# Language ids packed in the opening, and read into registers in fours

## The chip, the cores and the metric

The kernel runs on one core of a Trainium2 chip. Its engines work side by side, each through its own instructions in a fixed order: TensorE (PE in the profile, with its weight loads apart as PEld), VectorE (DVE), ScalarE (ACT), GpSimd (POOL) and SyncE (SP), which here issues transfers. They wait for each other by semaphores. The metric is the device time of one execution in microseconds, as the median of several runs.

## The reference

128 batches of 128 rows by 512 columns, float32. Each batch b has a language id from 0 to 8, and the id picks that batch's weights out of ten sets: a down projection W1 (512 to 128) with bias and relu, an up projection W2 (128 to 512) with bias, then a layer norm with a gamma and a beta of that language. Two residuals are added.

```python
w1 = W1[language_ids]
w2 = W2[language_ids]
h = jnp.einsum('bsh,bha->bsa', hidden_states, w1) + b1[language_ids][:, None, :]
h = jax.nn.relu(h)
adapted = jnp.einsum('bsa,bah->bsh', h, w2) + b2[language_ids][:, None, :]
x = hidden_states + adapted
mean = jnp.mean(x, axis=-1, keepdims=True)
var = jnp.mean(jnp.square(x - mean), axis=-1, keepdims=True)
normed = (x - mean) * jax.lax.rsqrt(var + LN_EPS)
return normed * gamma[language_ids][:, None, :] + beta[language_ids][:, None, :]
```

The output is the input x plus that result. The ids are data of the run, not known when the program is built.

## The kernel before

One batch is one tile of 128 by 512, and a loop written out over 128 batches passes it from engine to engine. TensorE transposes x (`transpose_x`, L479), multiplies by the batch's W1 (`down`, L502) and, after ScalarE's bias and relu (L510), by W2 (`up`, L524). VectorE adds the residual and sums (`residual`, L542), scales by gamma (`scale`, L608), takes the root through three small Newton steps (L579, L581, L584) and ends the batch (`finish`, L617). ScalarE copies the transposed tile (L483), squares (L565) and takes the root (L575). GpSimd adds b2 and beta to x ahead of time (`add_b2`, L489; `add_beta`, L496). SP loads x by pairs of batches (L188) and stores pairs (L621). Five PSUM banks hold the products of `up`; a bank is free again when `finish` of its batch has run.

The tables of all languages lie in the core's memory, so an id becomes an address: the offset of a slice of w2, beta_b, gamma_b, b2_b or w1. For that the engine that uses it needs the id in a register of its own. An engine gets it by a read (`TENSOR_LOAD`, L271), which stands in its order like any other instruction; one read can fill several registers.

The first 20 ids (NEAR) are read from the tile `lang`, four at a time, shortly before they are used. The other 108 are packed first: four ids of five bits, times 512, into one of 27 integers of the tile `packed`. VectorE does that with four small operations (`pack_ids`, L265 to L268). Each of the five engines then reads all 27 integers in one go (`read_packed`, L278) and keeps them in registers for the rest of the run; `lid` and `lid_h` take an id out by a shift and a mask.

The opening, up to batch 4, is a list of calls. After it the order on all engines follows a plan: every step is entered with a due time counted in batches, and the steps are sorted by it. Packing is due at 4.5, the long reads at 5.8 (SP), 6.7 (GpSimd), 7.6 (ScalarE), 8.5 (TensorE) and 9.4 (VectorE). In the opening VectorE also spreads the rows of beta and part of b2 over all 128 partitions (`shuffle_rows`, L397, 17 shuffles), and GpSimd's first `add_beta` waits for these.

Of the kernel before, what the change touches and what calls it, by code (L numbers as in the profile page):

```python
# [13 lines left out]
ET = mybir.EngineType  # L14
# [3 lines left out]
G = 4  # L18
# [125 lines left out]
def cond_resid_kernel(ctx: ExitStack, tc: tile.TileContext, x, itok, W1, b1, W2, b2, gamma, beta, out):  # L144
# [9 lines left out]
    B, S, H = x.shape  # L154
# [8 lines left out]
    def keep(ins):  # L163

        engine = ins.ins.engine
        if engine in last:
            tc.add_manual_dep(ins.ins, last[engine], behind, reason="kept order")
        last[engine] = ins.ins.name
        return ins
# [21 lines left out]
    def xb(b):  # L191
        return xs[b // X][:, b % X, :]


    ids = const.tile([1, B], I32, name="ids")
# [50 lines left out]
    lids, w1s = {}, {}  # L246
# [8 lines left out]
    NEAR, BITS = 20, 5  # L255
    FAR = (B - NEAR) // 4
    assert L <= 1 << BITS and H == 1 << 9 and NEAR % G == 0 and NEAR + 4 * FAR == B
    packed = const.tile([1, FAR], I32, name="packed")

    def pack_ids():  # L260

        def part(k):
            return lang[:, NEAR + k * FAR : NEAR + (k + 1) * FAR]

        keep(nc.vector.scalar_tensor_tensor(packed, part(3), float(1 << BITS), part(2), ALU.mult, ALU.add))  # L265
        for k in (1, 0):
            keep(nc.vector.scalar_tensor_tensor(packed, packed, float(1 << BITS), part(k), ALU.mult, ALU.add))
        keep(nc.vector.tensor_scalar(packed, packed, float(H), 0.0, ALU.mult, ALU.add))  # L268

    def read_ids(tile, engine, most, why):  # L270
        loads, vals = nc.values_load_multi_w_load_instructions(  # L271
            tile, engines=[engine], min_val=0, max_val=most, skip_runtime_bounds_check_because=why
        )
        for ins in loads:
            keep(ins)
        return vals

    def read_packed(engine):  # L278
        lids["far", engine] = read_ids(
            packed, engine, ((1 << 4 * BITS) - 1) * H, "four ids of 0..L-1 at five bits each, times H"  # L280
        )

    def near(b, engine):
        g = b // G
        if (g, engine) not in lids:
            lids[g, engine] = read_ids(
                lang[0:1, g * G : (g + 1) * G], engine, L - 1, "clamped on the chip to 0..L-1 above"
            )
        return lids[g, engine][b % G]

    def lid(b, engine):
        if b < NEAR:
            return near(b, engine)
        k, i = divmod(b - NEAR, FAR)
        v = (lids["far", engine][i] >> (BITS * k + 9)) & ((1 << BITS) - 1)
        return v.with_bounds(min_val=0, max_val=L - 1)

    def lid_h(b, engine):

        if b < NEAR:  # L300
            return near(b, engine) * H
        k, i = divmod(b - NEAR, FAR)
        v = lids["far", engine][i]
        if k:
            v = v >> (BITS * k)
        v = v & (((1 << BITS) - 1) * H)
        return v.with_bounds(min_val=0, max_val=(L - 1) * H, guaranteed_mod_val=0, out_of_modulus=H)
# [4 lines left out]
    def load_first(b):  # L312
        w1s[b] = wp.tile([P, KC, A], FP, tag="w1s", name=f"w1s_{b}")
        src = W1[bass.ds(lid(b, ET.SP), 1)].rearrange("o (p k) a -> p (o k a)", k=KC)
        keep(nc.sync.dma_start(out=w1s[b].rearrange("p k a -> p (k a)"), in_=src))
# [49 lines left out]
    def transpose_b1():  # L365
        b1p = p_h.tile([P, P], FP, tag="h", name="b1p")
        keep(nc.tensor.transpose(b1p[:, :L], b1r, ident[:L, :L]))
        keep(nc.vector.tensor_copy(b1T, b1p[:, :L]))
# [6 lines left out]
    def spread(r, copier):  # L375
        t = (beta_b, gamma_b, b2_b)[r // L]
        row = p_y.tile([P, H], FP, tag="y", name=f"row_{r}")
        pick_r = pick[:, r : r + 1].to_broadcast([96, P])
        keep(nc.tensor.matmul(row, lhsT=pick_r, rhs=parts[:96, :], start=True, stop=True))
        dst = t[:, r % L * H : (r % L + 1) * H]  # L380
        if copier is nc.scalar:
            keep(nc.scalar.copy(dst, row))
        else:
            keep(nc.vector.tensor_copy(dst, row))
# [53 lines left out]
    def load_rows(b):  # L438
        w1s[b] = wp.tile([P, KC, A], FP, tag="w1s", name=f"w1s_{b}")
        rows = W1[bass.ds(lid(b, ET.SP), 1)].rearrange("o (i k r) a -> i (o r) k a", i=4, k=KC)  # L440
        for i in range(4):
            keep(nc.sync.dma_start(out=w1s[b][32 * i : 32 * (i + 1)], in_=rows[i]))
# [21 lines left out]
    def stage_w1(b):  # L464
        w1s[b] = wp.tile([P, KC, A], FP, tag="w1s", name=f"w1s_{b}")
        gpsimd = turn(b) == "c"
        v = lid_h(b, ET.Pool if gpsimd else ET.Activation)
        src = w1.rearrange("p l k a -> p (l k a)")[:, bass.ds(v, KC * A)]
        dst = w1s[b].rearrange("p k a -> p (k a)")
        keep(nc.gpsimd.tensor_copy(dst, src) if gpsimd else nc.scalar.copy(dst, src))  # L470

    def transpose_x(b):
        pxs[b] = p_x.tile([P, KC, P], FP, tag="xT", name=f"pxT_{b}")
        for k in range(KC):
            if b < EARLY:
                cols = xb(b).rearrange("s (p k) -> s k p", k=KC)[:, k, :]
            else:
                cols = xb(b)[:, k * P : (k + 1) * P]
            keep(nc.tensor.transpose(pxs[b][:, k, :], cols, ident))  # L479

    def copy_xT(b):
        xT[b] = tp.tile([P, KC, P], FP, tag="xT", name=f"xT_{b}")
        keep(nc.scalar.copy(xT[b], pxs.pop(b)))  # L483

    def add_b2(b):
        if b2_on_gpsimd(b):
            rs[b] = rp.tile([P, H], FP, tag="r", name=f"r_{b}")
            v = lid_h(b, ET.Pool)
            keep(nc.gpsimd.tensor_tensor(rs[b], xb(b), b2_b[:, bass.ds(v, H)], ALU.add))  # L489

    def add_beta(b):
        g, j = divmod(b, 2)
        if g not in os:
            os[g] = op.tile([P, 2, H], FP, tag="o", name=f"o_{g}")
        v = lid_h(b, ET.Pool)
        keep(nc.gpsimd.tensor_tensor(os[g][:, j, :], xb(b), beta_b[:, bass.ds(v, H)], ALU.add))  # L496
# [11 lines left out]
    def relu(b):  # L508
        hT[b] = tp.tile([P, P], FP, tag="hT", name=f"hT_{b}", bufs=5)
        keep(nc.scalar.activation(hT[b], phs.pop(b), AF.Relu, bias=b1T[:, bass.ds(lid(b, ET.Activation), 1)]))  # L510
# [228 lines left out]
    def spin(n, width):  # L739
        idle = p_s.tile([P, H], FP, tag="s", name="idle")  # L740
        for _ in range(n):
            keep(
                nc.tensor.matmul(
                    idle[:, :width], lhsT=ones, rhs=ones[:, 0:1].to_broadcast([P, width]), start=True, stop=True
                )
            )
# [3 lines left out]
    def x_turn(b):  # L750
        transpose_x(b)
        copy_xT(b)
# [3 lines left out]
    spread(10, nc.scalar)  # L756
    spin(1, H)
    x_turn(0)
    transpose_b1()
    spread(11, nc.scalar)  # L760
    for n in (0, G):
# [16 lines left out]
    relu(2)  # L778
    spread(18, nc.scalar)
    spread(19, nc.scalar)  # L780
    add_beta(0)
    add_beta(1)
    spread(20, nc.scalar)
# [13 lines left out]
    def at(when, step, *args):  # L797
        plan.append((when, len(plan), step, args))
# [39 lines left out]
    for g in range(E // 2 - 1):  # L838
        b = 2 * g
# [13 lines left out]
            at_pair(g, when("scale", b) + 0.001, lid, b + G, ET.DVE)  # L853
        at_pair(g, when("store", b), store, g)

    at(4.5, pack_ids)
    for n, engine in enumerate((ET.SP, ET.Pool, ET.Activation, ET.PE, ET.DVE)):
        at(4.5 + 1.3 + 0.9 * n, read_packed, engine)

    for _, _, step, args in sorted(plan, key=lambda step: step[:2]):  # L860
        step(*args)
# [185 lines left out]
```

## Time and profile before

| | us |
|---|---|
| median of 3 runs | 303.61 |
| lowest and highest | 302.27, 303.68 |
| profiled execution | 303.65 |
| its span, first to last instruction | 300.9 |

| engine | busy us | share of the span |
|---|---|---|
| TensorE | 290.9 | 97% |
| VectorE | 291.2 | 97% |
| ScalarE | 273.4 | 91% |
| GpSimd | 276.2 | 92% |

Times inside the profile count from the first instruction. Reads into registers, register arithmetic and the issue of transfers are not counted as busy, so an engine that stands still for a read shows as idle. What the profile names as the end of an idle time is the semaphore that came last, which need not be the cause. The profiled execution is 2.75 us longer than its span.

### The profile page before, as it was taken

The page shows a single profiled execution, that of the slowest core. Times are in us where ns is not written, and L with a number is a line of the kernel's source. Part 1 is how long each engine was busy: PE and PEld are TensorE (multiplying, and loading weights), DVE is VectorE, ACT ScalarE, POOL GpSimd, SP SyncE. Part 2 cuts the span into 40 slices and gives each one's busy share as a digit, 9 for nine tenths or more (in the row PEclk, how much of TensorE's full clock was granted, in tenths as well). Part 3 has the DMA queues.
Part 4 walks back from the last instruction along what each step waited for, and adds up shares of the span by engine and source line. Part 5 has one row for each costly group of instructions (what it writes and reads, how often), then busy time and mean ns, then how long its engine had stood idle before and what let it go on. Part 6 is the DMA issues. An engine that isn't in the chain of part 4 may idle for free. (4 is left out here: it accounts for less than half of the span.)

```text
span 300.9 us, 8471 instructions
## 1 busy us (share of the span) xinstructions
PE 290.9 (97%) x1779; PEld 216.2 (72%) x1779; DVE 291.2 (97%) x780; ACT 273.4 (91%) x760; POOL 276.2 (92%) x238
## 2 busy tenths in 40 slices
PE   7998899999999999999999999999999999999993
PEld 3866587777767787777777777777777777777760
DVE  5999999999999999999999999999999999999995
ACT  4975688999999999999999999999999999899992
POOL 1196998999999999999999999999999999999982
PEclk9999999999999999999999999999999999999999
DMA  6999999969779898859975997949976898993816
GB/s 230 390 387 365 323 337 360 376 200 261 259 235 304 253 405 262 319 177 319 370 249 220 257 394 263 342 140 321 392 236 243 260 343 286 290 367 117 278 42 238
DMA packets 62260, 85.80 MB, mean 285 GB/s; under 512 B 4186, under 2 KB 26213, under 8 KB 62211
## 3 DMA queue, kind: packets, MB, share of 16 engines
q1 hardware_dynamic: 62150, 85.23, 83.8%
q8 instruction: 15, 0.25, 0.3%
q14 instruction: 35, 0.28, 0.3%
q10 hardware_dynamic: 60, 0.05, 0.1%
HBM read 51.71 MB, written 33.55 MB: 283 GB/s over the span
## 5 line engine op out<-in xcount | busy, mean ns | idle before, releaser
L496 POOL TENSOR_TENSOR o<-x,beta_b 128x512 f32<-128x512 f32 x121 | 151.9, 1278 | 15.4 <-DVE beta_b L397 12.7
L502 PEld LDWEIGHTS ph<-xT,w1s 128*128 128x128 f32 x1024 | 126.9, 192 | 13.4 <-ACT hT L510 8.3
L502 PE MATMUL ph<-xT,w1s 128*128 128x128 f32 x1024 | 135.4, 275 | 0.1
L489 POOL TENSOR_TENSOR r<-x,b_b 128x512 f32<-128x512 f32 x83 | 105.0, 1278 | 2.2 <-DVE part L581 1.6
L524 PE MATMUL py<-w,hT 128*128 x196 | 100.6, 596 | 1.5 <-DVE o L617 1.4
L479 PEld LDWEIGHTS pxT<-ident,x 128*128 128x128 f32 x464 | 60.1, 151 | 54.3 <-issue 39.5
L608 DVE SCALAR_TENSOR_TENSOR py<-py,nmean,gamma_b 128x512 f32<-128x512 f32 x124 | 93.0, 755 | 0.2
L565 ACT ACTIVATE sq<-py,sum 128x512 f32<-128x512 f32 x124 | 86.2, 695 | 1.8 <-DVE py L542 0.9
L617 DVE SCALAR_TENSOR_TENSOR o<-py,rstd,o 128x512 f32<-128x512 f32 x116 | 85.2, 749 | 1.2
L483 ACT COPY xT<-pxT 128x512 f32<-128x512 f32 x116 | 68.5, 590 | 7.8 <-PE pxT L479 7.8
L479 PE MATMUL pxT<-ident,x 128*128 128x128 f32 x464 | 71.4, 277 | 1.6 <-ACT root L575 1.3
L542 DVE SCALAR_TENSOR_TENSOR py<-py,r 128x512 f32<-128x512 f32 x88 | 61.1, 694 | 0.1
L510 ACT ACTIVATE hT<-ph,b1T 128x128 f32<-128x128 f32 x128 | 47.8, 374 | 5.8 <-PE ph L502 3.1
L470 ACT COPY w1s<-w 128x512 f32 x80 | 48.8, 624 | 0.0
L524 PEld LDWEIGHTS py<-w,hT 128*128 128x128 f32 x196 | 30.1, 192 | 3.7 <-DVE o L617 2.1
L516 PE MATMUL py<-w,hT 128*128 x60 | 30.8, 595 | 0.0
L565 ACT ACTIVATION_READ_ACCUMULATOR sq<-py,sum 128x1 f32 x124 | 26.0, 210 | 0.0
L542 DVE SCALAR_TENSOR_TENSOR py<-py,b_b 128x512 f32<-128x512 f32 x30 | 20.8, 693 | 0.0
L575 ACT ACTIVATE root<-ssq,eps 128x2 f32<-128x2 f32 x62 | 17.0, 274 | 2.6 <-DVE o L617 2.1
L462 ACT COPY py<-x 128x512 f32<-128x512 f32 x30 | 18.0, 600 | 0.1
L556 ACT ACTIVATE nmean<-sum 128x2 f32<-128x2 f32 x61 | 13.1, 214 | 0.3 <-DVE rstd L584 0.2
L542 DVE DVE_READ_ACCUMULATOR py<-py,r 128x1 f32 x88 | 12.6, 144 | 0.0
(83 smaller groups left out, 155.6 us busy)
## 6 DMA issues: line engine op xcount, KB each, us to landing
x<-in_x_dram SPq DMA_DIRECT2D x64, 512.0 KB, 7.0
out_dram<-o SPq DMA_DIRECT2D x62, 512.0 KB, 6.3
w1s<-in_L_cond_W_dram SPq DMA_DIRECT2D x25, 256.0 KB, 7.3
w1s<-in_L_cond_W_dram SPq DMA_DIRECT2D x48, 64.0 KB, 4.1
x<-in_x_dram SPq DMA_DIRECT2D x48, 64.0 KB, 2.0
w<-in_L_cond_W_dram SPq DMA_DIRECT2D x4, 640.0 KB, 7.1
w<-in_L_cond_W_dram SPq DMA_DIRECT2D x1, 1792.0 KB, 9.9
w<-in_L_cond_W_dram SPq DMA_DIRECT2D x1, 768.0 KB, 5.3
```

Of the source, the lines that this page charges most:

```text
L470: keep(nc.gpsimd.tensor_copy(dst, src) if gpsimd else nc.scalar.copy(dst, src))
L479: keep(nc.tensor.transpose(pxs[b][:, k, :], cols, ident))
L483: keep(nc.scalar.copy(xT[b], pxs.pop(b)))
L489: keep(nc.gpsimd.tensor_tensor(rs[b], xb(b), b2_b[:, bass.ds(v, H)], ALU.add))
L496: keep(nc.gpsimd.tensor_tensor(os[g][:, j, :], xb(b), beta_b[:, bass.ds(v, H)], ALU.add))
L502: nc.tensor.matmul(phs[b], lhsT=w1s[b][:, k, :], rhs=xT_of(b, k), start=(k == 0), stop=(k == KC - 1))
L510: keep(nc.scalar.activation(hT[b], phs.pop(b), AF.Relu, bias=b1T[:, bass.ds(lid(b, ET.Activation), 1)]))
L524: keep(nc.tensor.matmul(ys[b], lhsT=hT[b], rhs=w2[:, bass.ds(v, H)], start=not m, stop=True))
L542: nc.vector.scalar_tensor_tensor(ys[b], ys[b], 1.0, r, ALU.mult, ALU.add, accum_out=sum_of(b))
L565: nc.scalar.activation(sq, ys[b], AF.Square, bias=col(sums, b), scale=-float(H), accum_out=col(ssqs, b))
L608: nc.vector.scalar_tensor_tensor(ys[b], ys[b], col(nmeans, b), gamma_b[:, bass.ds(v, H)], ALU.add, ALU.mult)
L617: nc.vector.scalar_tensor_tensor(o, ys[b], rstds[g][:, j : j + 1], o, ALU.mult, ALU.add)
```

## The change

Packing moves from the plan into the opening: VectorE does it after its copy of the four rows (`four_copies`, L392) and before its copy of b1 (`transpose_b1`, L368). GpSimd reads all 27 integers at once, ahead of its first `add_beta`. ScalarE, TensorE and VectorE read them in seven groups, six of four and one of three, with due times half a batch per id apart: from 6.5, 6.3 and 7.0 on, to 18.5, 18.3 and 19.0. SP has no due time of its own and reads a group when a load first needs an id of it. What is computed is the same, and so is every step not named here; each engine but GpSimd has six reads more.

```diff
-    def read_packed(engine):
-        lids["far", engine] = read_ids(
-            packed, engine, ((1 << 4 * BITS) - 1) * H, "four ids of 0..L-1 at five bits each, times H"
-        )
-
...
+    def far(b, engine):
+        k, i = divmod(b - NEAR, FAR)
+        g = NEAR // G + i // G
+        if (g, engine) not in lids:
+            lids[g, engine] = read_ids(
+                packed[0:1, i // G * G : min(i // G * G + G, FAR)],
+                engine,
+                ((1 << 4 * BITS) - 1) * H,
+                "four ids of 0..L-1 at five bits each, times H",
+            )
+        return k, lids[g, engine][i % G]
+
+    def far_at_once(engine):
+        vals = read_ids(packed, engine, ((1 << 4 * BITS) - 1) * H, "four ids of 0..L-1 at five bits each, times H")
+        for i in range(0, FAR, G):
+            lids[(NEAR + i) // G, engine] = vals[i : i + G]
+
     def lid(b, engine):
         if b < NEAR:
             return near(b, engine)
-        k, i = divmod(b - NEAR, FAR)
-        v = (lids["far", engine][i] >> (BITS * k + 9)) & ((1 << BITS) - 1)
+        k, v = far(b, engine)
+        v = (v >> (BITS * k + 9)) & ((1 << BITS) - 1)
         return v.with_bounds(min_val=0, max_val=L - 1)
...
     spin(1, H)
     x_turn(0)
+    pack_ids()
     transpose_b1()
     spread(11, nc.scalar)
...
     spread(18, nc.scalar)
     spread(19, nc.scalar)
+    far_at_once(ET.Pool)
     add_beta(0)
     add_beta(1)
...
-    at(4.5, pack_ids)
-    for n, engine in enumerate((ET.SP, ET.Pool, ET.Activation, ET.PE, ET.DVE)):
-        at(4.5 + 1.3 + 0.9 * n, read_packed, engine)
+    for n in range(0, FAR, G):
+        for engine, first in ((ET.Activation, 6.5), (ET.PE, 6.3), (ET.DVE, 7.0)):
+            at(first + n / 2, far, NEAR + n, engine)
```

In the lists that follow a row is one instruction of an engine's order, ahead of it its line; lines from 290 on are 11 higher in the changed kernel, and 13 at its end. On VectorE the packing stood behind the residual of batch 3 and ahead of the first Newton step; `py` is a batch's product in PSUM, `part` the Newton step's scratch. Before:

```order
L534 TENSOR_TENSOR py_437<-py_437,b_b 128x512
L542 SCALAR_TENSOR_TENSOR py_437,sum_457<-py_437,x_141 128x512
L265 SCALAR_TENSOR_TENSOR packed<-lang 1x27
L267 SCALAR_TENSOR_TENSOR packed<-packed,lang 1x27 x2
L268 TENSOR_SCALAR packed<-packed 1x27
L579 SCALAR_TENSOR_TENSOR part_507<-ssq_488,root_506 128x2
```

After, it stands in the opening, and the Newton step (now L590) follows the residual (L553) at once:

```order
L403 COPY four<-four_p 128x512
L265 SCALAR_TENSOR_TENSOR packed<-lang 1x27
L267 SCALAR_TENSOR_TENSOR packed<-packed,lang 1x27 x2
L268 TENSOR_SCALAR packed<-packed 1x27
L379 COPY b1T<-b1p 128x10
L408 STREAM_SHUFFLE beta_b<-four 128x512 x10
```

The four operations moved ahead of 17 shuffles and the first four batches; nothing else changed its place among them.

On TensorE the long read stood behind `up` of batch 6 (`py_801`) and ahead of the transpose of batch 9. Before:

```order
L271 TENSOR_LOAD lang
L502 MATMUL ph_795<-xT_697,w1s_167 128x128 x4
L524 ISA
L524 MATMUL py_801<-w_92,hT_766 128x512
L271 TENSOR_LOAD packed
L479 MATMUL pxT_868<-ident,x_169 128x128 x4
```

After, that place is free, and reads of four stand between other matmuls (`py_727` is batch 6 here):

```order
L490 MATMUL pxT_592<-ident,x_163 128x128 x4
L271 TENSOR_LOAD packed
L513 MATMUL ph_616<-xT_559,w1s_161 128x128 x4
...
L513 MATMUL ph_712<-xT_669,w1s_167 128x128 x4
L271 TENSOR_LOAD packed
L535 ISA
L535 MATMUL py_727<-w_92,hT_683 128x512
L490 MATMUL pxT_748<-ident,x_169 128x128 x4
```

One read of 27 became seven, of which the first two are shown; the first stands behind the transpose of batch 6's x.

On GpSimd the long read stood between the sums of batches 5 and 6 (`o_459`, `o_677`). Before:

```order
L489 TENSOR_TENSOR r_499<-x_163,b_b 128x512
L496 ISA
L496 TENSOR_TENSOR o_459<-x_148,beta_b 128x512
L271 TENSOR_LOAD packed
L496 ISA
L496 TENSOR_TENSOR o_677<-x_163,beta_b 128x512
```

After, it is the first read of all, ahead of the first sum:

```order
masks.py:199 AFFINE_SELECT ident<-ident 128x128
L271 TENSOR_LOAD packed
L271 TENSOR_LOAD lang
L507 ISA
L507 TENSOR_TENSOR o_430<-x_99,beta_b 128x512
```

The read moved past nine sums and three reads of `lang`.

More of the change, by code (lines that the diff above doesn't have):

```diff
@@ L301, in lid_h @@
             return near(b, engine) * H
-        k, i = divmod(b - NEAR, FAR)
-        v = lids["far", engine][i]
+        k, v = far(b, engine)
         if k:
```

## The prediction

> **What bounds the kernel now.** I read the table of busy time by stretches first, because an average over the span says nothing of one stage. Its columns are the stretch, its length, then busy time and instructions of PE, PEld, DVE, ACT and POOL, the granted clock, the share of the DMA engines and GB/s. The span stands ahead of it.
>
> ```profile
> span 300.9 us, 8471 instructions
> ...
> 25.50:33.00 7.50, 4.71 (x26) 3.06 (x25) 7.32 (x20) 3.51 (x11) 4.95 (x5) 1.00 1.09 358
> 33.00:40.00 7.00, 7.00 (x47) 5.59 (x47) 6.32 (x17) 5.36 (x15) 7.00 (x7) 1.00 1.07 312
> 50.00:60.00 10.00, 10.00 (x66) 7.53 (x65) 9.81 (x28) 9.74 (x28) 8.44 (x8) 1.00 1.02 388
> 60.00:80.00 20.00, 19.92 (x127) 15.08 (x126) 20.00 (x53) 19.02 (x55) 19.95 (x17) 1.00 0.80 241
> ```
>
> In the steady loop (60 to 80 us) three engines are full at once: TensorE 19.92, VectorE 20.00, GpSimd 19.95 of 20. All run fixed orders, so whatever holds up all three near the start is carried to the end, and what is taken away there is worth the least that the binding ones of them gain. The bad stretch after the opening is 25.5 to 33 us: TensorE does 4.71 us of work in 7.50 and so loses 2.79, while VectorE looks busy with 7.32. So I read the timeline of each engine there.
>
> ```profile
> 22.58 0.31 DVE L265 SCALAR_TENSOR_TENSOR packed<-lang 1x27 int32<-1x27 int32 x1
> 22.92 2.42 DVE L267 SCALAR_TENSOR_TENSOR packed<-packed,lang 1x27 int32<-1x27 int32 x2
> 25.38 0.17 DVE L268 TENSOR_SCALAR packed<-packed 1x27 int32<-1x27 int32 x1
> 25.47 0.14 DVE L579 SCALAR_TENSOR_TENSOR part<-ssq,root 128x2 f32<-128x2 f32 x1
> ...
> 34.07 0.16 DVE L579 SCALAR_TENSOR_TENSOR part<-ssq,root 128x2 f32<-128x2 f32 x1 [0.50 <-ACT xT L483]
> ```
> ```profile
> 22.82 1.26 POOL L489 TENSOR_TENSOR r<-x,b_b 128x512 f32<-128x512 f32 x1
> 24.04 1.26 POOL L496 TENSOR_TENSOR o<-x,beta_b 128x512 f32<-128x512 f32 x1
> 28.05 1.28 POOL L496 TENSOR_TENSOR o<-x,beta_b 128x512 f32<-128x512 f32 x1 [2.74 <-DVE o L617]
> ```
> ```profile
> 22.04 0.28 ACT L575 ACTIVATE root<-ssq,eps 128x2 f32<-128x2 f32 x1
> ...
> 25.22 0.59 ACT L483 COPY xT<-pxT 128x512 f32<-128x512 f32 x1 [0.44 <-PE pxT L479]
> 27.89 0.27 ACT L575 ACTIVATE root<-ssq,eps 128x2 f32<-128x2 f32 x1 [2.08 <-DVE o L617]
> ```
> ```profile
> 27.45 1.12 PE L524 MATMUL py<-w,hT 128*128 x2 [1.37 <-DVE o L617]
> ...
> 32.48 0.72 PE L479 MATMUL pxT<-ident,x 128*128 128x128 f32 x4 [1.32 <-ACT root L575]
> ```
>
> The number ahead is the start, then the duration; the bracket is idle time ahead and what the profile names as its end. VectorE spends 22.58 to 25.47 on packing: 2.89 us of "busy" that moves no batch on. The names in the brackets are not the whole cause, because reads into registers are not counted as busy. They stand in the view of the two tiles:
>
> ```profile
> L271 ACTq TENSOR_LOAD <-packed x1: 2175/2175/2175, 25.6 to 25.6; - x1
> L271 POOLq TENSOR_LOAD <-packed x1: 2259/2259/2259, 25.6 to 25.6; - x1
> L271 PEldq TENSOR_LOAD <-packed x1: 2392/2392/2392, 30.0 to 30.0; - x1
> L271 DVEq TENSOR_LOAD <-packed x1: 2322/2322/2322, 31.7 to 31.7; - x1
> L271 SPq TENSOR_LOAD <-packed x1: 2083/2083/2083, 40.9 to 40.9; - x1
> ...
> L271 SPq TENSOR_LOAD <-lang x5: 298/306/520, 3.1 to 36.8; - x5
> L271 PEldq TENSOR_LOAD <-lang x5: 332/345/522, 5.1 to 38.3; - x5
> L271 ACTq TENSOR_LOAD <-lang x5: 307/314/506, 9.7 to 38.6; - x5
> L271 DVEq TENSOR_LOAD <-lang x5: 346/590/1258, 18.6 to 52.5; - x5
> ```
>
> Columns: count, shortest/median/longest in ns, first and last start. ScalarE and GpSimd both begin their long read at 25.6, when the packing has ended, and stand for 2.08 and 2.74 us. TensorE waits 1.37 us at 27.45 for a PSUM buffer that VectorE frees late (the packing), and 1.32 us at 32.48 behind its own read of 30.0 to 32.4. VectorE's read, from 31.7, covers itself behind queued work but for 0.50 us.
>
> **The change, part by part.** Packing, away from its old place: VectorE gains 22.58 to 25.47, 2.89 us. What follows it is ready by then: ScalarE writes the root that the 25.47 row reads from 22.04 to 22.32.
>
> Packing, in its new place: it stands between the copy of the four rows and the bias copy.
>
> ```profile
> 7.32 0.17 DVE L368 COPY b1T<-b1p 128x10 f32<-128x10 f32 x1 [1.22 <-PE b1p L367]
> ...
> 14.16 4.98 POOL L496 TENSOR_TENSOR o<-x,beta_b 128x512 f32<-128x512 f32 x4 [12.70 <-DVE beta_b L397]
> ```
>
> VectorE idles 1.22 us just there. The first packing step took 0.31; the two after it 2.42 together, 1.21 each. They end at 25.34; GpSimd's instructions of 22.82 and 24.04, as long as they, end at 24.08 and 25.30, and the step of 0.17 us ran after GpSimd had gone quiet. So I take 0.31 as the price with GpSimd quiet, and GpSimd does nothing for 12.70 us here: 3 x 0.31 + 0.17 = 1.10 us, inside the 1.22. Cost 0; the other end, with the old 2.89, is 2.89 - 1.22 = 1.67 us of later shuffles. The Trainium skill, "SBUF — State Buffer", section "Who interferes with whom", states that a VectorE instruction with two SBUF inputs contends with a GpSimd instruction that reads SBUF, and that the later one is blocked for the whole instruction; the ends just shown agree, and by that rule too the cost is 0.
>
> GpSimd's read of 27 now waits for the packing at about 7.3 and takes 2.26, with some 0.3 for its near ids behind it: done near 10, ahead of 14.16. Cost 0; the cover is 4 us of waiting for VectorE's shuffles. Its stall of 2.74 at 28.05 goes.
>
> ScalarE's and TensorE's long reads become seven reads of four or three, about 0.31 and 0.34 us each. None needs to wait: the packing is long over. The near reads of the same size show the exposure. The last one on TensorE starts at 38.3:
>
> ```profile
> 38.38 1.02 PE L524 MATMUL py<-w,hT 128*128 x2
> 39.24 0.64 PE L479 MATMUL pxT<-ident,x 128*128 128x128 f32 x4
> ```
>
> No idle time stands behind it, since a matmul of 1.02 us covers 0.34. So 7 x 0 on TensorE; the far end is 7 x 0.34 = 2.4. ScalarE did 3.51 us of work in 7.50 and 5.36 in 7.00: even 7 x 0.31 = 2.2 us, spread to about 50 us, stays in its slack. TensorE gains its 2.79.
>
> VectorE's long read, with 0.50 us exposed, becomes seven as well, and this is the uncertain term. The near reads on this engine reach 1.258 us. The last, at 52.5, ends here:
>
> ```profile
> 52.90 0.75 DVE L608 SCALAR_TENSOR_TENSOR py<-py,nmean,gamma_b 128x512 f32<-128x512 f32 x1
> 53.84 0.16 DVE L584 SCALAR_TENSOR_TENSOR rstd<-part,root 128x2 f32<-128x2 f32 x1 [0.18 <-DVE py L608]
> ```
>
> It exposed 0.18. So seven cost 0 to 1.3 us; I take 0.1 each, 0.7, since most stand just behind an operation of 0.7 us. VectorE's gain: 2.89 + 0.50 - 0.7 = 2.7.
>
> SP loses a read of 2.08 us at 40.9, ahead of the first store and the load of batches 20 and 21, and gets seven of 0.3 ahead of later weight loads. These loads wait far longer for TensorE to free a buffer:
>
> ```profile
> SPq L442 <- PE ph L502: 20.0, 9, 4.1
> ```
>
> That is 20.0 us in 9 waits, so the price is 0.
>
> Sum: GpSimd 2.74, TensorE 2.79, VectorE 2.7. GpSimd idles 1.56 us between 50 and 60 (8.44 of 10), so it doesn't bind by then; the two others give 2.7. The profiled execution took 303.65 us, 2.75 more than its span, and stands 0.04 above the median of 303.61. 303.65 - 2.7 = 300.95, told as 301.0.
>
> **The rivals.** First, the transfers. The DMA engines are full (1.02 to 1.09) up to 60 us, so loads cannot land earlier though work comes earlier. If it caught them, the gain would end there and the time stay near 303.6. A weight load of the opening:
>
> ```profile
> w1s<-in_L_cond_W_dram SPq DMA_DIRECT2D x25, 256.0 KB, 7.3
> ...
> 37.41 2.93 SPq L315 DMA_DIRECT2D w1s<-in_L_cond_W_dram  x1
> ...
> 50.86 1.06 PE L502 MATMUL ph<-xT,w1s 128*128 128x128 f32 x8
> ```
>
> Issued at 37.41 with 7.3 us to land, it is there at 44.7 and first used at 50.86: 6.1 us of room against 2.7, which speaks against the rival. 0.08.
>
> Second, the packing keeps its price. Then shuffles, and GpSimd's and VectorE's first work, come 1.67 us later, and 2.7 - 1.67 = 1.0 is left: 302.6. Against it speak the ends of the two slow steps; 0.08.
>
> Third, slower: VectorE's seven reads are exposed in full. Its gain without reads is 3.39, so the point is 3.39 / 7 = 0.48 us a read. At the median of 0.590 they cost 4.1, and the time is 303.65 + 0.7 = 304.4; at 1.258, 8.8 and 309. For it speaks that VectorE has no slack in the loop; against it that a read of 2.322 exposed 0.50 and one of 1.258 exposed 0.18. 0.10. The same on TensorE would cost its far end of 2.4 and leave 0.4 (303.3), no slower; 0.02. The Trainium skill, "DMA: Bandwidth & Descriptors", section "Latency and other measured facts", gives a `tensor_load` a floor of about 600 ns and has loads bundled to spread it, which speaks against seven reads in place of one: by it VectorE would pay an estimated 7 x 0.6 = 4.2 us, a time of 304.5. The rows of 298 to 346 ns on all engines lie under that floor.
>
> **How the numbers follow.** Forecast 0.72: 301.0, by its own ends 300.3 (VectorE's reads free, a gain of 3.4, if the others follow) to 301.5 (its reads 1.3, a gain of 2.1). The packing (302.6) lies inside the range; the transfers' full loss, TensorE's exposed reads and slower, 0.20 together, lie outside. The three runs of before are 1.4 us apart, so I reach 0.5 below the lowest and 0.3 above the highest end that I keep. Range 299.8 to 302.9. A measurement of this kernel tells about 0.5%, 1.5 us, from no change. Faster by more: 0.72. Within: packing, transfers and TensorE's reads, 0.18. Slower: 0.10.
>
> **What would show it.** Right: packing near 6 to 7.3 us, its steps 0.3 us each; GpSimd's read over before 14 us; no idle of 1 us or more on TensorE, ScalarE and GpSimd between 22 and 33 us; TensorE's stretch from 38 us shifted 2.7 to 3 us earlier and the same shift at 280. Wrong: packing steps of 1.2 us with GpSimd quiet; idle of 0.3 us or more on VectorE behind each read; TensorE or ScalarE waiting for a DMA between 35 and 60 us; a shift that is there at 40 and gone at 80.

## The result, and the profile after

The changed kernel takes 300.85 us as the median of its runs (300.57 to 300.86); the kernel before, beside it, 303.36 (302.27 to 303.68). The ratio is 0.9921, with a 95% interval of 0.9895 to 0.9948. Measured a second time, among the experiments, it was 0.9948 (0.9931 to 0.9966), 301.09 us. So the change saves 1.6 to 2.5 us, and the forecast of 301.0 with a range of 299.8 to 302.9 holds. Four executions of 338 to 1071 us, three of the kernel before and one of the changed kernel, are left out of all ratios.

Less of that than it seems lies inside the span. The profiled execution took 300.83 us with a span of 299.1, so 1.73 us lie outside the span, against 2.75 before. The span alone is 1.8 us shorter. And that execution of the kernel before was a long one: in 54 others, on three chips, its span was 299.7 to 301.4 us, with medians of 300.4 to 300.6 by chip, and 1.8 to 2.9 us lay outside. On the chip where both kernels ran most often the median spans are 300.4 and 299.3, so 1.1 us apart.

The same table of busy time by stretches as for the kernel before (columns: stretch, length, busy time and count of PE, PEld, DVE, ACT and POOL, granted clock, share of the DMA engines, GB/s), of the changed kernel:

```profile
span 299.1 us, 8487 instructions
...
25.50:33.00 7.50, 7.50 (x49) 5.85 (x48) 7.42 (x22) 5.74 (x18) 7.50 (x7) 1.00 1.09 355
...
40.00:50.00 10.00, 9.85 (x61) 7.08 (x59) 9.90 (x27) 8.18 (x24) 8.91 (x9) 1.00 1.08 360
50.00:60.00 10.00, 8.96 (x55) 6.69 (x56) 8.53 (x23) 8.28 (x24) 9.99 (x9) 1.00 0.95 365
```

From 25.5 to 33 us TensorE and GpSimd are now full: 7.50 of 7.50 each, against 4.71 and 4.95. The loss that the prediction wanted to remove is gone entirely. But a new one stands from 50 to 60 us: TensorE 8.96 against 10.00 before, VectorE 8.53 against 9.81, ScalarE 8.28 against 9.74.

The view of the packed tile shows both halves of the story (columns: engine, operation, count, shortest/median/longest in ns, first and last start in us):

```profile
L271 PEldq TENSOR_LOAD <-packed x7: 329/332/2119, 22.1 to 48.8; - x7
L271 ACTq TENSOR_LOAD <-packed x7: 305/310/2265, 23.3 to 49.7; - x7
L271 DVEq TENSOR_LOAD <-packed x7: 338/344/2224, 24.4 to 50.2; - x7
...
L271 POOLq TENSOR_LOAD <-packed x1: 2446/2446/2446, 6.9 to 6.9; - x1
```

GpSimd's long read runs from 6.94 to 9.39 us, far ahead of its first sum. The reads of the other three engines have medians of 310 to 344 ns, but on each engine the longest lasts over 2.1 us, nearly as long as the old read of 27. Taken one by one they are (duration in ns, start in us):

```
TensorE   333 @22.1   329 @26.5   330 @30.9   330 @35.2   332 @39.5   1253 @43.3   2119 @48.8
ScalarE   310 @23.3  ...                      305 @39.4    997 @44.2               2265 @49.7
VectorE   351 @24.4  ...                      342 @41.1    885 @47.7               2224 @50.2
```

The last two of each engine are the slow ones. The seventh reads three integers, the others four.

VectorE's timeline in the opening of the changed kernel (start, duration, then the instruction; in brackets the idle time ahead and what the profile names as its end), and one row further on:

```profile
5.41 0.69 DVE L403 COPY four<-four_p 128x512 f32<-128x512 f32 x1 [0.90 <-PE four_p L401]
6.12 0.18 DVE L265 SCALAR_TENSOR_TENSOR packed<-lang 1x27 int32<-1x27 int32 x1
6.33 0.38 DVE L267 SCALAR_TENSOR_TENSOR packed<-packed,lang 1x27 int32<-1x27 int32 x2
6.74 0.17 DVE L268 TENSOR_SCALAR packed<-packed 1x27 int32<-1x27 int32 x1
7.32 0.17 DVE L379 COPY b1T<-b1p 128x10 f32<-128x10 f32 x1 [0.41 <-PE b1p L378]
...
20.31 0.70 DVE L545 TENSOR_TENSOR py<-py,b_b 128x512 f32<-128x512 f32 x1 [0.47 <-issue]
...
23.04 0.15 DVE L590 SCALAR_TENSOR_TENSOR part<-ssq,root 128x2 f32<-128x2 f32 x1
```

Packing takes 6.12 to 6.91, 0.79 us in place of 2.89, and the copy of b1 still starts at 7.32: the price is nil. The Newton step that stood at 25.47 stands at 23.04. That is 2.43 us earlier and not 2.89, since a wait of 0.47 us has appeared at 20.31.

The stop at about 50 us that ends a part of the gain, on TensorE, ScalarE and VectorE of the changed kernel:

```profile
47.58 1.06 PE L513 MATMUL ph<-xT,w1s 128*128 128x128 f32 x8
...
51.02 1.13 PE L513 MATMUL ph<-xT,w1s 128*128 128x128 f32 x8 [1.08 <-ACT sq L576]
```
```profile
52.03 0.59 ACT L494 COPY xT<-pxT 128x512 f32<-128x512 f32 x1 [1.28 <-issue]
```
```profile
52.54 0.75 DVE L628 SCALAR_TENSOR_TENSOR o<-py,rstd,o 128x512 f32<-128x512 f32 x1 [1.47 <-issue]
```

Each of the three engines idles just as its seventh read ends: 48.8 + 2.12 = 50.9 on TensorE, 49.7 + 2.27 = 52.0 on ScalarE, 50.2 + 2.22 = 52.4 on VectorE. The profile names a semaphore for one and "issue" for two; only the view of the reads shows the cause.

How many microseconds earlier ScalarE's relu of a batch runs than in the kernel before, by the starts in the two traces (below, the shift):

```
batch                        5      8     10     14     16     17     40     80    127
changed kernel            0.12   3.65   3.65   3.60   3.28   1.87   2.01   2.02   1.93
```

The gain is made between batches 5 and 8 (22 to 33 us), and half of it is given back between batches 14 and 17. From there it stands still to the end. The shift counts from the one trace of before, whose span lies 0.3 to 0.5 us above its medians, so as a gain its last value is too large by about as much; between the kernels below it can be compared as it stands. So two questions are left: what made 3.65, more than forecast, and why did the seventh read cost what the first six did not?

### The profile page after: what moved, and what is told of

It reads as the page before. It is cut to its first block, busy times and chain, and to the rows that moved or that the text cites. A ratio compares the mean times of both kernels' runs of the same rounds, so it can differ in the third digit from the quotient of the medians.

```text
span 299.1 us, 8487 instructions
## 1 busy us (share of the span) xinstructions
PE 290.8 (97%) x1779; PEld 216.3 (72%) x1779; DVE 288.9 (97%) x780; ACT 273.4 (91%) x760; POOL 276.3 (92%) x238
## 5 line engine op out<-in xcount | busy, mean ns | idle before, releaser
L507 POOL TENSOR_TENSOR o<-x,beta_b 128x512 f32<-128x512 f32 x121 | 153.6, 1304 | 12.6 <-DVE beta_b L408 12.6
L500 POOL TENSOR_TENSOR r<-x,b_b 128x512 f32<-128x512 f32 x83 | 106.7, 1305 | 2.9 <-DVE part L592 2.2
L490 PEld LDWEIGHTS pxT<-ident,x 128*128 128x128 f32 x464 | 60.2, 151 | 52.5 <-issue 38.0
L553 DVE SCALAR_TENSOR_TENSOR py<-py,r 128x512 f32<-128x512 f32 x88 | 60.7, 690 | 0.0
L553 DVE SCALAR_TENSOR_TENSOR py<-py,b_b 128x512 f32<-128x512 f32 x30 | 20.6, 687 | 0.0
L553 DVE DVE_READ_ACCUMULATOR py<-py,r 128x1 f32 x88 | 12.3, 139 | 0.0
```

The source lines that it names most:

```text
L553: nc.vector.scalar_tensor_tensor(ys[b], ys[b], 1.0, r, ALU.mult, ALU.add, accum_out=sum_of(b))
```

## The experiments

My first theory was that a read of a few integers is slow when it falls among the first stores (SP's first store is issued at 40.9 us). Its rival was that three integers cost more than four, wherever the read stands. The ratios are to runs of the kernel before on the same chip. Their medians are 302.38 for the first four experiments; 302.67 for both mendings, the changed kernel again, the reads alone and GpSimd busy from the start; and 302.91 for the other four.

**Reads earlier.** The step of the due times is halved, so the last group comes at about 36 us.

```diff
-            at(first + n / 2, far, NEAR + n, engine)
+            at(first + n / 4, far, NEAR + n, engine)
```

> The changed kernel, but the seven groups are read a quarter of a batch per id apart, so that the last is due at batch 12.3 to 13 in place of 18.3 to 19. Theory 'stores' (a read is slow while stores are being taken out of the core's memory, which begins near 41 us): all reads of packed ids on TensorE, ScalarE and VectorE last 0.30 to 0.45 us, the idle of 1.1 to 1.5 us near 51 us is gone, and the time is 299.4 to 299.8 us. Theory 'three' (the last group is slow because it holds three integers): its read still lasts 2.1 to 2.3 us, now near 36 us, and the time is 300.5 to 301.2.

Measured: 299.57 us, ratio 0.9892 (0.9874 to 0.9910), span 297.9. Its view of the packed tile:

```profile
L271 PEldq TENSOR_LOAD <-packed x7: 327/331/771, 22.1 to 35.2; - x7
L271 ACTq TENSOR_LOAD <-packed x7: 305/310/702, 23.6 to 36.4; - x7
L271 DVEq TENSOR_LOAD <-packed x7: 340/342/752, 24.7 to 38.2; - x7
```

The longest read, still the seventh, falls from over 2.1 to 0.70 to 0.77 us. It is dearer than a read of four, but no engine stands for it: TensorE is busy 9.99 of 10 from 40 to 50 us and 10.00 from 50 to 60. The shift of 3.3 us stays to the last batch.

**Four in place of three.** A 28th integer, zero, pads the last group; due times as in the changed kernel.

```diff
-    packed = const.tile([1, FAR], I32, name="packed")
+    padded = const.tile([1, FAR + 1], I32, name="packed")
+    packed = padded[:, :FAR]
...
+        keep(nc.vector.memset(padded, 0))
...
-                packed[0:1, i // G * G : min(i // G * G + G, FAR)],
+                padded[0:1, i // G * G : i // G * G + G],
```

> The changed kernel with a 28th integer (zero) behind the 27, so that the last group holds four; due times as in the changed kernel. 'Three': the last read lasts 0.33 us, the idle near 51 us is gone, 299.4 to 299.8 us. 'Stores': the last reads still last about 2 us, 300.5 to 301.2 us.

Measured: 299.38 us, 0.9883 (0.9863 to 0.9902), span 297.8. The seventh reads, at 48.8, 49.7 and 50.3 us, take 913, 836 and 923 ns; the sixth on TensorE, at 43.3, takes 1252. So at the same place four integers cost less than half of three, yet nearly three times what four cost before 40 us. VectorE idles 0.32 us at 51.36 in place of 1.47, and 3.2 us of the shift stay. Each theory is half right: it takes the odd three and the place together to make 2.1 us.

**Reads later.** The groups of the changed kernel, due from 12.3 to 13 on, a quarter batch per id apart, so that they stand at 35 to 52 us.

```diff
-            at(first + n / 2, far, NEAR + n, engine)
+            at(first + 6 + n / 4, far, NEAR + n, engine)
```

> The changed kernel with the seven reads due at 12.3 to 19, a quarter of a batch per id apart, so that nearly all fall behind 41 us. 'Stores': most of the seven last 0.8 to 2.3 us on each engine, and the time is 302 to 307 us. 'Three': only the last is slow, 300.5 to 301.3 us.

Measured: 302.14 us, 0.9997 (0.9974 to 1.0021), span 300.4.

```profile
L271 PEldq TENSOR_LOAD <-packed x7: 329/910/1871, 34.8 to 50.4; - x7
L271 ACTq TENSOR_LOAD <-packed x7: 304/759/1767, 36.0 to 50.5; - x7
L271 DVEq TENSOR_LOAD <-packed x7: 340/699/1207, 37.7 to 51.5; - x7
```

Now the medians rise too. TensorE stands 1.18 us at 44.5 and 1.28 at 51.1; the shift grows to 3.95 us at batch 10 and falls to 0.8. So the time shows nothing of the gain any more: it hangs on where the reads stand.

**Packing alone.** The kernel before, with only the packing moved to the opening; the reads of 27 keep their due times.

```diff
     x_turn(0)
+    pack_ids()
     transpose_b1()
...
-    at(4.5, pack_ids)
```

> The kernel before with the packing moved to the opening and nothing else; the reads of 27 stay where they were. By the terms of the forecast TensorE gets back the 1.37 us in which it waited for VectorE, and keeps the 1.32 us behind its own long read, as ScalarE and GpSimd keep their stalls of about 2 us: 302.0 us, in a range of 301.4 to 302.6. If the packing were the whole of it, 300.9; if the reads were, 303.4.

Measured: 300.88 us, 0.9954 (0.9932 to 0.9977), span 298.9. The 302.0 expected missed; it came out as stated for the case that the packing is the whole of it.

```profile
L271 POOLq TENSOR_LOAD <-packed x1: 2258/2258/2258, 20.5 to 20.5; - x1
L271 ACTq TENSOR_LOAD <-packed x1: 2157/2157/2157, 25.1 to 25.1; - x1
L271 PEldq TENSOR_LOAD <-packed x1: 2364/2364/2364, 28.1 to 28.1; - x1
```
```profile
27.38 0.27 ACT L575 ACTIVATE root<-ssq,eps 128x2 f32<-128x2 f32 x1 [1.72 <-DVE py L608]
27.99 1.16 PE L502 MATMUL ph<-xT,w1s 128*128 128x128 f32 x8 [0.72 <-ACT hT L510]
...
30.55 0.72 PE L479 MATMUL pxT<-ident,x 128*128 128x128 f32 x4 [0.55 <-ACT sq L565]
```

GpSimd's read starts at 20.5, lasts as long as before, and the stall of 2.74 us is gone all the same: the read no longer waits for the packing and lies beside GpSimd's queued sums. What made the stall was thus that the read had to start late, at 25.6 us behind GpSimd's last queued sum, which ended at 25.3, and not its length alone. On TensorE 0.72 + 0.55 us of idle are left of 1.37 + 1.32. The relu of the last batch runs 1.97 us earlier, as far as with the whole change (1.93). The split of the reads, as the change places it, adds nothing to the end.

**Both mendings.** The changed kernel with the earlier due times and the padded group.

> The earlier due times and the 28th integer together: the last read is one of four and falls near 36 us. If both shortened the same wait, as each alone removed the idle near 51 us, little is left to win: every read of packed ids on TensorE, ScalarE and VectorE 0.30 to 0.36 us, the time 0 to 0.4 us under that of either alone, about 0.988 of the kernel before. If they removed different waits the gains add, and it is 0.985.

Measured: 298.94 us, 0.9887 (0.9860 to 0.9915), span 297.1.

```profile
L274 PEldq TENSOR_LOAD <-packed x7: 327/331/333, 21.9 to 35.1; - x7
L274 ACTq TENSOR_LOAD <-packed x7: 304/305/309, 23.2 to 36.3; - x7
L274 DVEq TENSOR_LOAD <-packed x7: 339/342/352, 24.2 to 37.7; - x7
```
```profile
50.00:60.00 10.00, 10.00 (x63) 7.40 (x63) 10.00 (x28) 9.51 (x28) 10.00 (x9) 1.00 1.02 391
```

All 21 reads take 0.304 to 0.352 us, and TensorE, VectorE and GpSimd are full from 50 to 60 us. The shift is 3.67 us at batch 8 and 3.88 at the last. This version beats the kernel before and, with an interval below that of the next experiment, the changed one.

**The changed kernel again**, on the chip of the run above, as its neighbour.

> The changed kernel itself once more, on the same chip as the others of this set: 0.992 of the kernel before, 1.0 to 1.3 us over the early and padded one. If the differences between sets came from the chip, it is within 0.3 us of it.

Measured: 301.09 us, 0.9948 (0.9931 to 0.9966), span 299.2. The seventh reads take 2.17 to 2.31 us, TensorE then idles 1.26 us, ScalarE 1.35 and VectorE 1.50; the shift falls from 3.65 to 1.77 and ends at 1.84. The loss at 50 us belongs to the kernel, not to one execution. Mending it was worth 301.09 - 298.94 = 2.15 us on one chip, more than the 1.0 to 1.3 expected.

**Reads alone.** Packing back at 4.5 and GpSimd's read at 6.7, but the seven groups due as in the change.

```diff
-    pack_ids()
...
-    far_at_once(ET.Pool)
...
+    at(4.5, pack_ids)
+    at(6.7, far_at_once, ET.Pool)
```

> Reads in fours on ScalarE, TensorE and VectorE, SP's on demand, but packing where it was (due 4.5) and GpSimd's read of 27 behind it. Terms: the packing still takes 2.89 us of VectorE and stops GpSimd and ScalarE until about 25.5, TensorE's 1.37 us wait stays, its 1.32 goes; 1.1 us of waiting on the last read comes. By that 0.2 us or so is won: 303.0, or 0.999 of the kernel before, between 0.996 and 1.002. If the gain were all in the reads: 0.992.

Measured: 304.32 us, 1.0053 (1.0031 to 1.0075), span 303.7 in the profiled execution, which at 305.51 was the slowest of nine. The forecast of hardly any change missed. TensorE and the packing in this run:

```profile
26.33 1.13 PE L513 MATMUL ph<-xT,w1s 128*128 128x128 f32 x8 [3.38 <-DMA w1s<-in_L_cond_W_dram]
```
```profile
L267 DVE SCALAR_TENSOR_TENSOR packed<-packed,lang x2: 175/682/1189, 24.1 to 25.4; 1x27 int32<-1x27 int32 x2
L265 DVE SCALAR_TENSOR_TENSOR packed<-lang x1: 1217/1217/1217, 22.9 to 22.9; 1x27 int32<-1x27 int32 x1
```

TensorE's first group is due at 6.3, ahead of the end of the packing at 25.7. Its read starts at 25.77, and TensorE stands 3.38 us for it. The name in the bracket, a transfer, is again not the cause. The granted clock from 25.5 to 33 us was 0.77 in this run, against 1.00. The experiment therefore says that the early reads need the early packing, but not what the split is worth.

**Reads alone, each engine in its old place.** As before, with groups due from 7.6, 8.5 and 9.4, a quarter batch per id apart, and the last one padded.

```diff
...
-        for engine, first in ((ET.Activation, 6.5), (ET.PE, 6.3), (ET.DVE, 7.0)):
-            at(first + n / 2, far, NEAR + n, engine)
+        for engine, first in ((ET.Activation, 7.6), (ET.PE, 8.5), (ET.DVE, 9.4)):
+            at(first + n / 4, far, NEAR + n, engine)
```

> Short reads alone, without the waiting that spoilt the first attempt: packing due at 4.5 as before, GpSimd's read of 27 behind it, and on ScalarE, TensorE and VectorE seven reads of four (a 28th integer of zero), the first where the read of 27 stood (7.6, 8.5, 9.4), a quarter of a batch per id apart. TensorE gets back the 1.32 us behind its long read and keeps the 1.37 us of waiting for the packing: 0.9955 of the kernel before (0.9935 to 0.998). If the two halves only work together, 0.999 to 1.0; if the reads are the larger half, 0.992 or less.

Measured: 301.48 us, 0.9974 (0.9956 to 0.9991), span 299.7.

```profile
26.57 1.13 PE L538 MATMUL py<-w,hT 128*128 x2 [0.77 <-DVE o L631]
```
```profile
27.18 1.27 POOL L510 TENSOR_TENSOR o<-x,beta_b 128x512 f32<-128x512 f32 x1 [2.96 <-DVE py L622]
```

GpSimd's stall of the kernel before is back (2.96 us, with its read at 24.7 behind the packing), and so is most of VectorE's slow packing (22.76 to 24.67, with one step of 1.19 us). The shift is 2.4 us at batch 8 and 1.3 at the end. Three of VectorE's reads, two of `packed` and one of `lang`, at 41.7 to 44.6, take 0.96 to 1.32 us. So each part has a worth of its own: by the shift at the last batch 2.0 us for the packing, 1.3 here, and 3.9 together where no read falls among the stores. The 1.3 is no clean price of the split: the packing was about 0.9 us shorter here than before, which the reads did not do, and the three slow reads count against it. With the packing in the opening, the reads that both mendings have add 3.88 - 1.97 = 1.9 us to it.

**GpSimd busy from the start.** To see whether the packing is cheap because GpSimd is quiet, GpSimd does seven sums that nobody uses.

```diff
+    busy = const.tile([P, H], FP, name="busy")
+    keep(nc.gpsimd.memset(busy, 0.0))
+    for _ in range(7):
+        keep(nc.gpsimd.tensor_tensor(busy, busy, busy, ALU.add))
```

> The changed kernel with seven sums of 128x512 on GpSimd, of no use, beside the packing in the opening. If the two slow steps of the packing waited for GpSimd's instructions, they last up to 1.27 us each again (0.17 us with GpSimd quiet), and the first shuffle starts 1 to 2 us after 7.4 us. If their price was their own place, they stay at 0.17.

Measured: 306.11 us, span 304.4, by one run. It missed its aim: the sums end at 10.0 us, and the packing comes only at 12.0, with 0.17 us a step, because VectorE's earlier steps were held up.

```profile
1.95 1.02 DVE L235 TENSOR_TENSOR both<-ident 96x32 f32<-96x32 f32 x1 [0.77 <-POOL ident masks.py:199]
...
4.26 1.06 DVE L250 TENSOR_SCALAR wrap<-ids 1x128 int32<-1x128 int32 x1
```

Those two took 0.19 and 0.21 us without the sums.

**GpSimd busy during the packing.** Three useless sums that read the tile which VectorE copies just ahead of the packing, so they start with it.

```diff
+    busy = const.tile([P, H], FP, name="busy")
+    for _ in range(3):
+        keep(nc.gpsimd.tensor_tensor(busy, fours[0], fours[0], ALU.add))
```

> The changed kernel with three sums of 128x512 on GpSimd, of no use, that start when the copy of the four rows has ended, so just with the packing. Theory 'GpSimd's instruction blocks it': of the four packing steps two or three last 0.9 to 1.3 us, the first shuffle starts 1.2 to 2 us later than 7.41, and the time is 0.9965 to 0.9985 of the kernel before, the second rival's price. If the price came from the place: 0.17 us a step, the first shuffle at 7.4, 0.992 to 0.995.

Measured: 301.31 us, 0.9945 (0.9923 to 0.9966), span 299.6.

```profile
6.34 1.13 DVE L267 SCALAR_TENSOR_TENSOR packed<-packed,lang 1x27 int32<-1x27 int32 x2
7.50 0.90 DVE L268 TENSOR_SCALAR packed<-packed 1x27 int32<-1x27 int32 x1
```
```profile
6.18 3.31 POOL L772 TENSOR_TENSOR busy<-four 128x512 f32<-128x512 f32 x3 [4.72 <-DVE four L403]
```

With GpSimd at work the packing ends at 8.40 and not at 6.91, and the first shuffle comes 1.0 us later. Not every step is slow, only the first of the two of L267 and the last. The record of each instruction shows which: a step that starts while a sum is under way ends 0.03 to 0.04 us after that sum (at 7.26 behind a sum that ends at 7.22, and at 8.40 behind one that ends at 8.37), and the two that start just ahead of a sum, at 6.13 and 7.29, take 0.175. The span is 0.4 to 0.5 us longer than the changed kernel's two; the times of the two kernels are not told apart, and 0.9945 lies below the 0.9965 to 0.9985 expected. That GpSimd's sums slow these small steps is shown, and so is the reason for the low price in the opening.

**No early stores.** The changed kernel without the stores of the first eight pairs; those 16 batches are not written.

```diff
-        at_pair(g, when("store", b), store, g)
+        if g >= 8:
+            at_pair(g, when("store", b), store, g)
```

> The changed kernel without the stores of the first eight pairs of batches (those 16 batches of the output are not written), so that no store is under way until about 60 us. 'Stores': the reads between 43 and 51 us last 0.30 to 0.36 us where they hold four and 0.7 to 0.8 where they hold three, and the idle near 51 us is gone. If a read late in the plan is slow for another reason, they last 0.9 to 1.3 and 2.1 to 2.3 us as in the changed kernel.

Measured, by one run: 299.94 us, span 297.5.

```profile
L271 PEldq TENSOR_LOAD <-packed x7: 328/332/773, 22.1 to 48.8; - x7
L271 ACTq TENSOR_LOAD <-packed x7: 305/309/705, 23.4 to 49.8; - x7
L271 DVEq TENSOR_LOAD <-packed x7: 341/345/749, 24.5 to 50.0; - x7
L271 SPq TENSOR_LOAD <-packed x7: 298/912/2778, 60.2 to 154.3; - x7
```
```profile
40.00:50.00 10.00, 9.99 (x63) 7.49 (x62) 9.90 (x27) 8.36 (x24) 8.79 (x8) 1.00 1.08 361
```

The reads stand at the same places as in the changed kernel, the DMA share is the same 1.08, now of loads alone, and yet the seventh reads take 0.71 to 0.77 us and the sixth 0.31 to 0.35. The first store is at 65.29 us here, and SP's reads, which come later, reach 2.78 again. So it is the stores that slow a read, not full transfers as such. The shift stays at 3.55 us.

**A read of 28.** What does a read cost by its size? The kernel with packing alone, its long reads padded from 27 to 28 integers.

```diff
...
-            packed, engine, ((1 << 4 * BITS) - 1) * H, "four ids of 0..L-1 at five bits each, times H"
+            padded, engine, ((1 << 4 * BITS) - 1) * H, "four ids of 0..L-1 at five bits each, times H"
```

> Packing in the opening and one long read per engine as in the run with the packing alone, but of 28 integers (the last is zero) in place of 27. If a read costs 0.08 us and 0.25 us for each whole four and for each integer left over (27: nine of these, 28: seven), the long reads last 1.8 to 1.9 us instead of 2.16 to 2.36. If it costs 0.08 us an integer, they last 2.2 to 2.45.

Measured, by one run: 300.87 us, span 298.3. The span is 0.6 shorter than with 27; the time, 300.88 there, is the same.

```profile
L274 POOLq TENSOR_LOAD <-packed x1: 1794/1794/1794, 20.5 to 20.5; - x1
...
L274 PEldq TENSOR_LOAD <-packed x1: 1873/1873/1873, 27.8 to 27.8; - x1
L274 DVEq TENSOR_LOAD <-packed x1: 1894/1894/1894, 29.8 to 29.8; - x1
```

One integer more, and the read is half a microsecond shorter (TensorE 2.364 to 1.873). The durations fit 0.08 us and 0.25 for each piece, where a piece is four integers or a single left over: four is one piece, 0.33; three are three, 0.83 by this (0.70 to 0.77 measured); 28 are seven, 1.83 (1.64 to 1.89); 27 are six and three, 2.33 (2.07 to 2.39). GpSimd's 2.45 in the changed kernel is the first read on its engine, and those are longer: of four, 0.49 to 0.61 us. The pieces are a fit to reads of 3, 4, 27 and 28 integers; reads of one or two were not measured.

## Why the prediction was right, and where it was not

The sign, the time and the range held. The steps did not all.

**Packing in the opening, 1.10 us inside 1.22 of idle.** Right, and cheaper: 0.79, with the copy of b1 at 7.32 as before. The 0.31 a step was itself misread as a price beside a quiet GpSimd: in the kernel before, a sum ran from 21.58 to 22.85, and the first step ended right behind it, at 22.89. Undisturbed, the step takes 0.175. The reason, GpSimd being quiet, stood the test with three useless sums. The rival that the packing keeps its price fell. The Trainium skill, "SBUF — State Buffer", section "Who interferes with whom", has the one of two contending VectorE and GpSimd instructions that issues first keep the shared ports for its whole length, with the other blocked. The ends of the steps agree: those that start under a sum of 1.1 to 1.3 us end 0.03 to 0.04 us after it, and take 0.90 to 1.22 us where most of the sum was still to come.

**GpSimd's long read done near 10 us.** Right: 9.39, ahead of a first sum at 14.07, and no idle behind it to 33 us. The 2.74 us did go, but packing alone removes them with the read left where it was.

**No idle of 1 us between 22 and 33.** Right: TensorE and GpSimd are full from 25.5 on, and ScalarE's longest wait is 0.96.

**The shift at 38 us, 2.7 to 3.** Mis-sized: 3.65. The term is TensorE's 2.79, which was its idle time. TensorE's transposes before and, below, after show what the stops cost it:

```profile
24.55 0.63 PE L479 MATMUL pxT<-ident,x 128*128 128x128 f32 x4
...
28.41 0.63 PE L479 MATMUL pxT<-ident,x 128*128 128x128 f32 x4
...
32.48 0.72 PE L479 MATMUL pxT<-ident,x 128*128 128x128 f32 x4 [1.32 <-ACT root L575]
```
```profile
24.46 0.64 PE L490 MATMUL pxT<-ident,x 128*128 128x128 f32 x4
...
26.68 0.64 PE L490 MATMUL pxT<-ident,x 128*128 128x128 f32 x4
...
28.91 0.64 PE L490 MATMUL pxT<-ident,x 128*128 128x128 f32 x4
```

With no stop a batch follows the last by 2.22 to 2.23 us. Before, the two distances are 3.86 and 4.07, so the stops cost 1.63 and 1.84, 3.47 together, while the brackets show 1.37 and 1.32. The ends of matmuls in the profile are modelled, and its idle time falls short of what a stop costs. With the 0.12 us that batch 5 is ahead, that is 3.6 of the 3.65. VectorE's `finish` is 3.3 us ahead by then, close to its terms before its reads are charged, 2.89 + 0.50 = 3.39.

**VectorE's packing, 2.89.** 2.43 at the Newton step, since 0.47 us of idle has come in at 20.31. In most other runs with the early packing it is 0.5 to 1.0, in two of them 0.13 or none. I haven't settled where it comes from. It costs little at the end: the version with both mendings has it ahead of batch 6 too and is 3.88 us earlier.

**Reads: 0 on TensorE, 0.1 for each of VectorE's.** This is the step that failed. Six of seven cost next to nothing on any engine that binds (TensorE idles 0.15 us in all from 20 to 50 us), and the seventh costs 1.08 us on TensorE, where I took 0, and 1.47 on VectorE, where I took 0.7 in all and 1.3 as the far end. I counted seven equal reads, "of four or three, about 0.31 and 0.34 us each". The trace of before had a warning: VectorE's near reads of 952 ns at 44.2 us and 1258 at 52.5, against 336 on TensorE at 38.3. I took the long ones for VectorE's own; they were the ones made among the stores. That three integers cost more than four, no row of before could have shown. "The same shift at 280" was therefore wrong: 1.93 us at the last batch.

**Each of VectorE's reads exposed (rival, 304.4).** Fell as stated; one read is. The Trainium skill, "DMA: Bandwidth & Descriptors", section "Latency and other measured facts", which gives a `tensor_load` a floor of about 600 ns, does not agree with the rows here: while no store runs, four integers take 295 to 407 ns on all engines in all runs, apart from each engine's first read, which takes 493 to 605.

**Transfers catch up (rival, 303.6).** Fell. No engine waits for a transfer between 35 and 60 us, and with both mendings 3.88 us come through to the end.

**The sum.** 2.7 us were forecast within the span, and 1.8 came by the two traces, 1.1 by the median spans on one chip. The profiled execution of before had 2.75 us outside its span, and the changed kernel's two had 1.73 and 1.74. That these last, 1 us, made up for the missing 0.9 is luck; over the profiled executions of all kernels the part outside was 1.7 to 2.75 us, and I found no cause for it. The start of the sum helped too: 303.65 is 0.7 to 1.3 us above the medians of the kernel before beside the experiments, 302.38 to 302.91. So a start that was too high made up for a gain that was forecast too large. The forecast is better judged by the span, and there it was 0.9 us too good by the traces and 1.6 by the medians. The seventh read accounts for more than that: with the reads mended, the gain in the span is 300.9 - 297.1 = 3.8 by the traces, 3.3 by the medians.

## What to carry to other kernels

In these runs a read into registers cost nothing where its data were long there and enough work was queued ahead of it: 0.33 us on TensorE, and even 2.26 on GpSimd. Look at each read's own duration and place, since a group's median hides the one that stalls three engines at once. Read small integers in whole fours, and before the stores begin; either alone brought most of it here. Moving the work that others wait for (here four small steps on VectorE, to a place where GpSimd is quiet) gave as much as the whole change did; the second part paid only after its last read was put right.

## What the hardware showed unexpectedly

- A read of 28 integers is shorter than one of 27 (1.64 to 1.89 us against 2.07 to 2.36 in two kernels that differ in the padding alone), and one of four shorter than one of three (0.33 against 0.70 to 0.77). The sizes fit a cost of 0.20 to 0.25 us for each left-over integer, about as much as for a group of four.
- Stores under way slow many of these reads: on TensorE, ScalarE and VectorE to as much as 1.3 us for four and 2.5 for three, though some stay as they were. Loads that fill the transfers as much (share 1.08) do not. Why stores do it isn't shown.
- GpSimd's sums hold up VectorE's small steps for about 1 us, also those with a single tensor as input (0.17 to 0.90 and 0.21 to 1.06). Which of several steps is hit depends on where each starts against the sums: in the run with the reads alone the first and second packing steps took 1.22 and 1.19 us, each ending 0.04 us behind a sum, and the third, behind the last sum, 0.175; before, it was the second and third.
